# Cross attention on one core: the whole program as one list of words, and the second batch's output in 33 products

## The chip, the cores and the metric

The kernel runs on one core of one Trainium2 chip. A core has five engines that run side by side, each through its own queue of instructions: TensorE (PE; matrix products, its weight loads are listed apart as PEld), VectorE (DVE), ScalarE (ACT), GpSimd (POOL) and SyncE (SP), which here does nothing but issue transfers between DRAM and the on-chip memory SBUF. Products land in PSUM, eight banks of 128 partitions by 512 numbers of 32 bits. The metric is the device time of one execution in microseconds (us).

## What is computed

Two batches of 2048 tokens with 640 channels attend to 154 rows of context with 1024 channels each: 77 of text and 77 of image, with key and value weights of their own and a softmax of their own. There are 20 heads of 32 channels. All is float32.

```python
q = split_heads(x @ Wq.T)
k, v = split_heads(text @ Wk.T), split_heads(text @ Wv.T)
k_ip, v_ip = split_heads(ip @ Wk_ip.T), split_heads(ip @ Wv_ip.T)
out = merge_heads(attend(q, k, v)) + merge_heads(attend(q, k_ip, v_ip))
return out @ Wo.T + bo + x
# attend: softmax(q @ k.T / sqrt(32)) @ v
```

## The kernel before

The matrices lie transposed, with the channels on the 128 partitions. 640 channels are five chunks of 128 (four heads each), 2048 tokens are four blocks of 512 (two halves, `sub`, of two blocks, `h`). A unit `u` (0 to 19) is one batch, one chunk and one half: 1024 tokens in eight groups of 128. It is worked in three groups (`R0`, `R1`, `R2`: three, three and two of the eight).

What a unit does, by the letters that the order of work uses:
- `q` (`queries`, L218): five products of 512 columns into one bank; `cq` (L229) copies it to SBUF.
- `k`, `v` (`project_kv`, L132): keys and values of a chunk, for both batches at once, eight products; `ck`, `cv` copy them. `SQ` (L146) turns v in squares of 32 by VectorE, `VS` (`spread_v`, L152) spreads them over the partitions by 16 small transfers.
- `R` (`scores`, L246), `K` (L261, ScalarE copies the scores into the tile `pb`), `M` (L271, maxima, VectorE), `S` (L277, subtraction, GpSimd), `E` (L283, exponential, ScalarE), `D` (L289, sums and their reciprocals, VectorE), `N` (L297, multiplication, GpSimd), `T` (L303, transposition in squares of 32, VectorE).
- `A` (`attend`, L308): probabilities by values for both halves of a chunk, into four banks; `CA` (L332) copies them into the tile `aT`.

The first batch's output runs between the units of the second batch, the second batch's output after the last attention. For the first 512 output channels and the first 512 input channels it is a scheme of seven products for eight (`product`, L474): channels split in 2 x 2, tokens of a block in halves of 256, with sums of weights (`sum_w`, L365: five, on GpSimd) and of tokens (`sum_t`, L407: four of 512 columns for a block, on GpSimd). Each product is four instructions of 256 columns, four of the seven have two more for the fifth chunk (L491). `take_product` (L500) adds a bank to the residual tile, whose rows were loaded from x, with the bias at the first time. The last 128 output channels are plain products (`last_chunk`, L459, in two parts: `p` ahead of the last attention, the fifth chunk behind it) with `store_last` (L469). In the trace each product is two instructions.

The order of the body is written out as strings, one for each engine and kind of unit (`ORDERS`, L562), merged by a loop that writes a word out as soon as all that it needs has been written (L908). The transfers are issued by SP, one queue, in the order in which the code meets them: the next block of x when a block's last query has been written (`load_next`, L197), eight `VS` transfers behind it, `Wo` and the first residuals behind those of chunk 4 (L168). The last stage is a list by itself (L917 to L939).

Of the kernel before, what the change touches and what calls it, by code (L numbers as in the profile page):

```python
# [19 lines left out]
def kernel(  # L20
# [41 lines left out]
    SCALE = 1.0 / float(D) ** 0.5  # L62
    NP = B * NC
# [50 lines left out]
    loaded, used = [], set()  # L114

    def load_w(upto=len(wlist)):

        while len(loaded) < upto:
            n = len(loaded)
            if n >= len(wslots) and n - len(wslots) not in used:  # L120
                return
            src, c = wlist[n]
            w = wslots[n % len(wslots)]
            nc.sync.dma_start(
                out=w, in_=src[:, ts(c, P)].rearrange("(k p) o -> p k o", p=P)
            )
            loaded.append(w)
# [4 lines left out]
    def project_kv(n, out):  # L132

        load_w()
        t = n % 2
        for k in range(NCC):
            nc.tensor.matmul(  # L137
                keys_in(out), loaded[n][:, k, :], cT[:, k, :, t, :], start=(k == 0), stop=(k == NCC - 1)
            )
        used.add(n)  # L140
# [9 lines left out]
    rest = []  # L150

    def spread_v(q):  # L152


        spread_rest(len(rest))
        for g in range(G):
            for r in range(G):
                rest.append((q, g, r))
        spread_rest(G * G // 2 if q == NC - 1 else None)
        if q == NC - 1:  # L160
            rest.extend(["x", "wo"])

    def spread_rest(n=None):
        for _ in range(len(rest) if n is None else min(n, len(rest))):
            w = rest.pop(0)
            if w == "x" and n is None:
                return
            if w == "wo":  # L168
                nc.sync.dma_start(out=wo, in_=WoT.rearrange("(c p) o -> p c o", p=P))
                for part in PARTS:  # L170
                    fetch(0, part)
            if w in ("x", "wo"):
                continue
            q, g, r = w
            nc.sync.dma_start(  # L175
                out=v4s[q % 2][r * D : (r + 1) * D, g].rearrange("p k d -> p (k d)"),
                in_=squares(q)[g * D : (g + 1) * D],
            )
# [18 lines left out]
    def load_next(u, h):  # L197

        _, b, c, _ = step_of(u)
        n = place_of(u, h)  # L200
        if b == 0 and (c < NC - 1 or n == XROOM):
            return
        m = late.index((u, h)) + XROOM if b else n
        if m < len(late):
            v, g = late[m]
            tokens = ds(S + (step_of(v)[3] * NH + g) * TB, TB)
            nc.sync.dma_start(out=xs[n], in_=xT[:, tokens].rearrange("(k p) t -> p k t", p=P))
            spread_rest()
# [20 lines left out]
    def take_queries(u, h, pq):  # L229
        qT = qpool.tile([P, TB], F32, tag="qT", name=f"qT_{u}_{h}")  # L230
        nc.scalar.copy(qT, pq)  # L231
        qTs[(u, h)] = qT
# [38 lines left out]
    def maxima(u, s):  # L271
        n = GROUPS[s][1] * G
        mx = small.tile([P, n, 2], F32, tag=f"mx{n}", name=f"mx_{u}_{s}")
        nc.vector.tensor_reduce(mx, rows_of(u, s), AX.X, ALU.max)  # L274
        maxs[s] = mx

    def subtract(u, s):  # L277
        n = GROUPS[s][1] * G
        nc.gpsimd.tensor_tensor(  # L279
            rows_of(u, s), rows_of(u, s), maxs[s].unsqueeze(3).to_broadcast([P, n, 2, L]), ALU.subtract  # L280
        )

    def exponential(u, s):  # L283
        e = keys_of(u, s).rearrange("p n g l -> p (n g) l")
        nc.scalar.activation(e, e, AF.Exp, scale=SCALE)  # L285
# [3 lines left out]
    def sums(u, s):  # L289
# [5 lines left out]
        rdens[s] = rden  # L295

    def normalise(u, s):  # L297
        n = GROUPS[s][1] * G
        nc.gpsimd.tensor_tensor(  # L299
            rows_of(u, s), rows_of(u, s), rdens[s].unsqueeze(3).to_broadcast([P, n, 2, L]), ALU.mult  # L300
# [225 lines left out]
    for k in (0, half):  # L526
# [4 lines left out]
        load_w(k // half + 1)  # L531
    for _ in range(NH * NC):
        load_x()
    load_w()
# [11 lines left out]
    for t in range(2):  # L546
# [3 lines left out]
        for b in range(B):  # L550
            nc.scalar.copy(kT[:, 0, b, t, :], keys_in(ps)[:, b])

    ORDERS = {  # L562
        "0": (
            "1010", "430",
            "R0 R1 R2 F2 F0 F1",
            "K0 K1 K2 E0 E1 E2 C0 C2 C1",
            "M0 C0 M1 M2 D0 D1 D2 T0 C2 C1",
            "S0 S1 S2 N0 N1 N2",
        ),
        "1": (  # L570
            "1000", "26647",
            "F0 R0 R1 F3 F2 R2 F4 F1",
            "C0 K0 K1 K2 C2 E0 C3 C4 E1 E2 C1",
            "SQ M0 M1 T1- C3 C4 M2 T2- D0 D1 C0 D2 T0 C2 C1",
            "S0 S1 S2 N0 N1 N2",
        ),
        "even": (
            "1101", "310",
            "R2 R0 F2 R1 F0 F1 AT",
            "K2 K0 K1 E0 C0 C2 E1 C1 E2 CA",  # L580
            "C0 M0 T1- M1 T2- M2 D0 C2 C1 D1 D2 T0",
            "S0 S1 S2 N0 N1 N2",
        ),
        "odd": (
            "0010", "05244",
            "R0 F3 F0 R2 R1 F4 F2 F1",
            "K0 C3 C0 K2 K1 E0 C2 E2 C4 E1 C1",
            "M0 C4 C1 T1- M2 M1 SQ C2 D0 T2- D2 C0 C3 D1 T0",
            "S0 S2 S1 N0 N2 N1",
        ),  # L590
        "8": (
            "1100", "502",
            "R2 R0 F1 R1 F2 F0 AT",
            "K2 K0 K1 C2 C1 E0 C0 E2 E1 CA",
            "M2 C1 M0 T2- T1- M1 C0 D0 D2 D1 T0 C2",
            "S2 S0 S1 N0 N2 N1",
        ),
        "9": (
            "1101", "020",
            "R0 F0 R2 R1 F2 F1",  # L600
            "C0 K0 K2 K1 E0 E2 C1 C2 E1",
            "SQ M0 T2- C1 C2 M2 M1 D0 T1- C0 D2 D1 T0",
            "S0 S2 S1 N0 N2 N1",
        ),
        "10": (
            "1001", "4110",
            "F1 R0 R2 F0 R1 AT F2 F3",
            "C1 K0 K2 C0 K1 CA E0 E2 E1",
            "T2- T1- M0 M1 M2 D0 C2 C3 D1 D2 T0",
            "G1 W0 S0 S2 S1 N0 W1 N1 N2",  # L610
        ),
        "11": (
            "1100", "335421",
            "R0 F1 R1 R2 F3 F2 F4 F0 F5",
            "K0 C1 K1 K2 E0 C0 E1 E2",
            "M0 C3 M1 M2 C4 T1- C2 D0 T2- D1 C5 D2 T0",
            "S0 G2 S1 G3 S2 N0 N2 N1 G4",
        ),
        "12": (
            "0000", "7605",  # L620
            "R1 F0 F2 R0 F1 R2 F3 AT",
            "K1 K0 C0 C1 K2 E0 E1 CA E2",
            "C2 T2- M0 T1- M1 C3 M2 D0 D1 T0 D2",
            "S0 S1 S2 N0 G1 N1 N2",
        ),
        "13": (
            "0011", "560574",
            "F1 R0 F3 R1 R2 F2 F4 F5 F0",
            "K0 C1 K1 K2 E0 E1 E2 C0",
            "C3 M0 M1 M2 C2 T2- D0 D1 C5 D2 C4 T0 T1-",  # L630
            "S0 S1 S2 N0 N1 N2 G3",
        ),
        "14": (
            "0000", "6540",
            "R2 F0 R1 F2 R0 F1 AT F3",
            "K2 K1 K0 C1 E2 E0 CA E1 C0",
            "M2 T1- T2- M0 M1 C2 D2 D0 C3 D1 T0",
            "S2 G2 S0 S1 G4 N0 N2 N1",
        ),
        "15": (  # L640
            "0000", "071365",
            "F5 R0 F4 R2 F2 R1 F1 F3 F0",
# [329 lines left out]
```

## Time and profile before

| what | us |
|---|---|
| median of three runs (lowest, highest) | 509.31 (509.28, 510.11) |
| span of the profiled execution | 506.7 |
| its time outside the span | not recorded for this execution; the median is 2.6 above the span |
| first query product starts | 4.4 |
| last attention starts, ends | 431.3, 436.8 |
| first output product behind it starts | 437.12 |
| last matmul ends | 502.97 |

How to read the profile: the page gives, for one execution, the busy time of each engine. "By stretches" cuts the span; a row has the busy time of TensorE, the weight loads, VectorE, ScalarE and GpSimd with their instructions in brackets, then the granted clock and the DMA share. The chain of work that ended last is followed back from the end; its pieces have a start and a length. The timeline merges neighbours of the same line: start, length from the first start to the last end, engine, line, operation, output<-inputs, shape, number. VectorE's and GpSimd's own lengths overlap a little with the next instruction's, so the distance from start to start is what one costs in a row.

### The profile page before, as it was taken

To read this page: it belongs to the slowest core of one execution; us is meant where nothing else is said; L and a number is where in the kernel's file an instruction comes from. 1 tells how busy PE (TensorE), PEld (TensorE's weight loads), DVE (VectorE), ACT (ScalarE), POOL (GpSimd) and SP (SyncE) were. 2 spreads that over 40 slices of the span, in tenths; PEclk is the share of its full clock that TensorE was granted. 3 is DMA by queue.
4 is the path that set the end of the run, shared out by engine and by line. 5 is a ranking of instruction groups with operands and counts; after the bars stand their busy time and mean duration, and the time that the engine had idled before them with its cause. 6 is when DMAs were issued, how large, how long until landed. Compare 5 with 4: busy or idle time off the path is not lost.

```text
span 506.7 us, 10153 instructions
## 1 busy us (share of the span) xinstructions
PE 498.3 (98%) x4270; PEld 321.0 (63%) x4270; DVE 391.9 (77%) x347; ACT 242.5 (48%) x423; POOL 395.0 (78%) x163
## 2 busy tenths in 40 slices
PE   9999999999999999999999999999999999999997
PEld 5657557557656565456565656554755775588885
DVE  0079999999899987958997997699899999333333
ACT  1266666666676566645545636454654750100000
POOL 0079999989989988899999997798899999940000
PEclk9999999999999999999999999999999999999999
DMA  8982621331362453885574485168323242641213
GB/s 274 357 210 61 159 69 46 86 92 46 92 185 74 112 198 116 284 314 145 159 237 124 131 260 158 53 178 292 110 72 95 86 162 65 225 147 62 84 41 104
DMA packets 71053, 73.03 MB, mean 144 GB/s; under 512 B 5600, under 2 KB 50912, under 8 KB 71008
## 3 DMA queue, kind: packets, MB, share of 16 engines
q1 hardware_dynamic: 70288, 71.67, 45.9%
q8 instruction: 33, 0.54, 0.5%
q10 hardware_dynamic: 720, 0.72, 0.4%
q14 instruction: 12, 0.10, 0.1%
HBM read 58.61 MB, written 10.49 MB: 136 GB/s over the span
## 4 chain that ended last, share of the span: by engine, by line
PE 86%; DMA 5%; POOL 4%; DVE 1%; SPq 1%; issue 1%; ACT 0%; DVEq 0%; POOLq 0%
PE bank L221 31%; PE bank L481 18%; PE bank L253 9%; PE bank L315 9%; PE bank L137 9%; PE bank L461 5%; PE bank L491 5%; DMA x<-in_x_dram 3%; DMA wo_ct<-in_L_xattn_Wo_dram 2%; POOL pb L299 2%; POOL pb L279 1%; SPq L175 1%; POOL x L384 1%; DMA acc<-in_x_dram 1%; PE bank L541 1%
## 5 line engine op out<-in xcount | busy, mean ns | idle before, releaser
L279 POOL TENSOR_TENSOR pb<-pb,mx 128x1848 f32<-128x1848 f32 (+1 forms) x60 | 175.4, 2941 | 45.3 <-DVE mx L274 45.1
L221 PE MATMUL bank<-x,wq 128*128 128x512 f32 x400 | 180.7, 601 | 0.1
L299 POOL TENSOR_TENSOR pb<-pb,rden 128x1848 f32<-128x1848 f32 (+1 forms) x60 | 175.0, 2939 | 5.2 <-DVE rden L294 5.2
L274 DVE TENSOR_REDUCE mx<-pb 128x24 f32<-128x1848 f32 (+1 forms) x60 | 109.6, 1845 | 33.0 <-ACT pb L265 32.8
L265 ACT COPY pb<-bank 128x462 f32<-128x462 f32 (+1 forms) x240 | 101.7, 535 | 59.3 <-PE bank L253 58.5
L221 PEld LDWEIGHTS bank<-x,wq 128*128 128x128 f32 x400 | 74.1, 191 | 85.0 <-issue 81.7
L292 DVE TENSOR_REDUCE den<-pb 128x24 f32<-128x1848 f32 (+1 forms) x60 | 110.4, 1840 | 17.3 <-ACT pb L285 16.9
L285 ACT ACTIVATE pb<-pb 128x1848 f32<-128x1848 f32 (+1 forms) x60 | 94.9, 1582 | 56.4 <-POOL pb L279 56.2
L306 DVE STREAM_TRANSPOSE pb<-pb 128x1920 f32<-128x1920 f32 (+1 forms) x60 | 114.8, 1923 | 2.1 <-POOL pb L299 2.1
L253 PEld LDWEIGHTS bank<-kT,qT 32*128 32x128 f32 x1280 | 47.4, 184 | 26.3 <-issue 18.0
L253 PE MATMUL bank<-kT,qT 32*128 32x154 f32 x1280 | 58.7, 306 | 0.7 <-ACT vT L899 0.4
L315 PE MATMUL bank<-pb,v 32*32 32x512 f32 x1600 | 55.8, 597 | 1.2 <-ACT pb L265 0.7
L481 PE MATMUL bank<-aT,wo_ct 128*128 128x256 f32 x192 | 47.6, 382 | 1.0 <-DVE acc L512 0.7
L137 PEld LDWEIGHTS bank<-wo_ct,aT 128*128 128x128 f32 x320 | 43.1, 188 | 4.2 <-issue 3.5
L315 PEld LDWEIGHTS bank<-pb,v 32*32 32x32 f32 x1600 | 30.7, 103 | 23.2 <-issue 11.8
L137 PE MATMUL bank<-wo_ct,aT 128*128 128x154 f32 x320 | 45.3, 295 | 0.0
L481 PEld LDWEIGHTS bank<-aT,wo_ct 128*128 128x128 f32 x192 | 36.0, 190 | 11.0 <-issue 3.8
L231 ACT COPY qT<-bank 128x512 f32<-128x512 f32 x40 | 23.1, 588 | 31.4 <-PE bank L221 31.4
L461 PE MATMUL bank<-aT,wo_ct 128*128 128x512 f32 x80 | 36.1, 597 | 0.0
L506 DVE SCALAR_TENSOR_TENSOR pb<-bank,bo_sb,pb 128x256 f32<-128x256 f32 x24 | 10.5, 479 | 26.9 <-PE bank L491 16.4
L491 PE MATMUL bank<-aT,wo_ct 128*128 128x256 f32 x96 | 28.6, 379 | 0.0
L506 DVE SCALAR_TENSOR_TENSOR acc<-bank,bo_sb,acc 128x256 f32<-128x256 f32 x40 | 17.0, 466 | 13.3 <-PE bank L491 6.6
(47 smaller groups left out, 286.2 us busy)
## 6 DMA issues: line engine op xcount, KB each, us to landing
x<-in_x_dram SPq DMA_DIRECT2D x20, 1280.0 KB, 6.9
x<-in_x_dram SPq DMA_DIRECT2D x21, 256.0 KB, 5.2
out_dram<-acc SPq DMA_DIRECT2D x19, 256.0 KB, 2.8
acc<-in_x_dram SPq DMA_DIRECT2D x16, 256.0 KB, 6.7
v<-vS SPq DMA_DIRECT2D x160, 20.0 KB, 1.8
pb<-in_x_dram SPq DMA_DIRECT2D x3, 1024.0 KB, 7.6
wq<-in_L_xattn_Wq_dram SPq DMA_DIRECT2D x9, 320.0 KB, 4.8
aT<-in_L_xattn_Wk_dram SPq DMA_DIRECT2D x5, 512.0 KB, 5.6
```

The costliest lines, as they stand in the source:

```text
L137: nc.tensor.matmul(keys_in(out), loaded[n][:, k, :], cT[:, k, :, t, :], start=(k == 0), stop=(k == NCC - 1))
L221: nc.tensor.matmul(pq, wqs[q % 3][:, k, :], xs[place_of(u, h)][:, k, :], start=(k == 0), stop=(k == NC - 1),)
L253: nc.tensor.matmul(ps[g][:, ts(t, 2 * L)], qTs[(u, h)][g * D : (g + 1) * D, ts(st, P)], kT[g * D : (g + 1) * D, c, b].rearrange("p t l -> ...
L265: nc.scalar.copy(keys_of(u, s)[:, :, g], ps[g][:, : n * 2 * L].rearrange("p (n l) -> p n l", n=n))
L274: nc.vector.tensor_reduce(mx, rows_of(u, s), AX.X, ALU.max)
L279: nc.gpsimd.tensor_tensor(rows_of(u, s), rows_of(u, s), maxs[s].unsqueeze(3).to_broadcast([P, n, 2, L]), ALU.subtract)
L285: nc.scalar.activation(e, e, AF.Exp, scale=SCALE)
L292: nc.vector.tensor_reduce(den, rows_of(u, s), AX.X, ALU.add)
L299: nc.gpsimd.tensor_tensor(rows_of(u, s), rows_of(u, s), rdens[s].unsqueeze(3).to_broadcast([P, n, 2, L]), ALU.mult)
L306: nc.vector.transpose(p, p)
L315: nc.tensor.matmul(pa[r][g * D : (g + 1) * D, :], v4s[q % 2][rows, g, k, :], zones[rows, :, g, k, :], start=(k == 0), stop=(k == NK - 1),)
L481: nc.tensor.matmul(part, w_of[m][:, kp, op], t_of(m, b, i)[:, kp], start=(op == kp == 0 and m in (1, 2, 5)), stop=(op == 1 and kp == 1 and ...
```

## The change

All that is in `ORDERS`, `OUTPUT` and the last list becomes one list of words, `SCHEDULE` (953 words), from which each engine's queue and SP's queue are written in that order. A word is one of the steps above with its unit (`R0.5`), `@` gives the bank or half of the banks. Loads are words as well: `LX` a block of x, `LQ` query weights, `LK` key and value weights, `LO` all of `Wo`, `LF` the first residuals. Up to the last attention the words are those of before in a somewhat different order. The scale 1/sqrt(32) moves from the exponential to the copy of the queries. `DIRECT` is empty, so the path for it is never taken.

The second batch's output for the first 512 output channels is a scheme of its own: weights as 4 x 5 squares of 128, tokens in two halves of 1024, 33 products in place of 40 plain ones. A product `F` is one weight square by 1024 tokens, written as two words of 512 columns. 24 weight sums `V` (40 instructions, on VectorE, into the first zone of `pb`) and 25 token sums `X` (1024 columns; 18 on GpSimd, `p`, and 7 on VectorE, `d`). Eight chains of products each gather in one bank per block, and are read on the way by `Y`, which adds or subtracts the bank to or from a residual tile (62 words); a product behind a `Y` goes on in the same bank. `z`, `yz` are the fifth chunk of the last 128 channels and its addition. Three of the four blocks' residuals are the last blocks of x, which still lie in SBUF; the fourth is loaded (`LA`). `LW` loads a part of `Wo` again that the first batch's scheme has overwritten.

The core of the diff:

```diff
@@ take_queries
-        nc.scalar.copy(qT, pq)
+        nc.scalar.mul(qT, pq, SCALE)
@@ exponential
-        nc.scalar.activation(e, e, AF.Exp, scale=SCALE)
+        nc.scalar.activation(e, e, AF.Exp)
@@ the lists
-    ORDERS = {
...
-    written = {None}
-    while any(queues):
...
+    SCHEDULE = (
+        "R0.0@1 R1.0@0 K0.0 K1.0 M0.0 R2.0@1 q.1.1@0 K2.0 LK.5 M1.0 S0.0 LK.4 M2.0 q.1.0@1 S1.0 E0.0 cq.1.1 "
...
+        "T2.0 VS.0.0 K0.2 M2.2 N2.1 M0.2 VS.0.1 N1.1 R1.2@1 T0.1 v.1.0@2 LF T2.1 S2.2 q.4.0@3 cv.1.0 K1.2 "
...
+        "N0.8 cv.4.0 D1.8 CA.3 R0.9@1 v.4.1@0 N2.8 T0.8 K0.9 N1.8 cv.4.1 M0.9 R2.9@0 R1.9@1 K2.9 q.10.1@0 "
+        "SQ.4 S0.9 K1.9 T2.8 VS.4.1 M2.9 M1.9 S2.9 E0.9 VS.4.0 q.11.0@3 T1.8 S1.9 E2.9 LX.12.0 cq.10.1 LO "
...
+        "R0.12@0 cm3.0 q.13.0@5 G5.1 E2.11 cm6.0 K0.12 G7.0 D2.11 N0.11 D1.11 m7.0 LX.14.0 VS.6.1 M0.12 N1.11 "
+        "q.13.1@6 cm7.0 D1.10 T1.11 N1.10 R2.12@0 LQ.9 LQ.8 q.14.0@7 K2.12 T0.11 N2.11 T1.10 m4.0 S0.12 T2.11 "
...
+        "T2.18 p.0@5 cm6.3 D0.19 S2.19 E1.19 D1.19 m7.3 N0.19 E2.19 p.1@4 cm7.3 LW D2.19 N1.19 T0.19 m4.3 "
+        "N2.19 T1.19 p.2@7 X.A.p@0 T2.19 cm4.3 V.P LA A.9@0 V.A V.Q V.G V.O V.M X.D.d@1 X.I.p@2 X.K.d@3 CA.9 "
+        "V.E F31.0@0 V.J V.U F31.1@1 V.T V.F V.L X.U.d@4 F0.0@0 z.2 V.B V.H V.S F0.1@1 V.X F25.1@2 V.R V.D "
+        "V.C z.0 X.S.d@5 z.3 Y6.1.10 X.L.p@6 z.1 yz.0 yz.2 F7.0@3 Y0.0.11 F7.1@5 X.T.p@7 yz.3 F25.0@7 Y0.1.11 "
+        "Y2.1.31 F23.0@0 Y6.0.10 X.O.p@8 F23.1@1 Y0.0.01 F20.1@2 Y2.1.21 Y0.1.01 F20.0@7 X.C.p@9 yz.1 F24.0@0 "
+        "Y6.1.11 F24.1@1 Y6.0.11 F15.1@5 V.N Y2.0.31 X.Q.p@10 F10.0@4 F10.1@6 Y3.0.21 F29.0@7 X.V.d@11 "
+        "F11.0@4 Y3.1.21 X.M.p@12 F1.0@0 Y2.0.21 F11.1@6 Y0.0.00 F29.1@2 Y6.0.21 X.G.p@13 Y3.0.20 F1.1@1 "
+        "Y3.1.20 F13.1@5 F6.0@0 V.V Y0.1.00 X.F.p@0 F15.0@3 Y2.1.11 F3.0@4 Y6.1.21 F13.0@3 X.B.d@4 F3.1@6 V.I "
+        "F30.1@2 Y3.0.00 X.J.p@5 Y3.1.00 F18.0@0 Y6.1.20 F18.1@1 V.W F30.0@7 X.W.d@3 F21.0@4 Y2.0.11 X.N.p@6 "
...
+        "F32.0@0 Y5.0.31 Y1.0.30 F9.1@6 Y1.1.20 F16.0@7 Y4.0.20 F9.0@7 Y5.1.21 Y1.1.30 F28.1@2 Y5.0.21 "
+        "F32.1@2 Y7.0.30 Y4.1.20 "
+    ).split()
@@ the scheme: sums of tokens A.., sums of weights A.., products (weight, tokens), chains
+    R_SUMS = (
+        "+01-21 +30+11 +21-31 +31+11 +10-00 +11-10 +30-31 +30+10 +01-00 +01-11 +01-D +21-I +30+C +G+J +D-I "
+        "+M-20 +20-L +E+N +40-41 +11-41 +11-40 +10-40 +C-40 +C-41 +V+20 "
+    ).split()
+    W_SUMS = (
+        "+01+30 -32-13 +10+02 +34-24 +03-01 +01+20 +30+31 +20-E +D-22 +03-A +13-I -32-02+12 +00-10-20 "
+        "-12-10-13 +00+01+02 +14-04-34 -P-11 +H+22+23 +32-J+33 +Q-22-24 -G-01+21-22 +U+03-23 +13-V-33 "
+        "+01-Q-03-21+22+23 "
+    ).split()
+    PRODUCTS = (
+        "04 41, 02 Q, K C, M 00, 30 E, B M, L 20, 34 S, W 30, D X, "
+        "H K, F O, A R, N 21, J N, P T, R D, G F, 11 V, S G, "
+        "Q U, O I, E J, C L, 04 S, T 40, I W, 32 P, U H, X 11, "
+        "V B, 10 A, 22 Y"
+    ).split(", ")
+    CHAINS = (
+        "0,31:+11 23:+01 1,24:+00 6,18:+10",
+        "4:-00 17:-20-30",
+        "7:-21-31 13,15:-11",
+        "10:+21 11:+20 3:+00 21:+01",
+        "14:-31 12:+00 28,32:+20",
+        "22:+01+31 9,16:+21",
+        "25:-10 20:-11 29:-21 30:-20 8:-30 19:-31",
+        "26:-21 2:-11 5:-31 27:-10-30",
+    )
...
+        n = int(text)
+        if n < 2:
+            flat = xs[XROOM].rearrange("p k t -> p (k t)")[:, ts(n, NH * TB)]
+        elif n < 4:
+            return aT[:, ds(NC * NHB + 2 * (n - 2), NH)]
+        else:
+            flat = pb_flat[:, ds(zone + (n - 4) * NH * TB, NH * TB)]
...
+    def add_part(o, ps, op):
+        t = sum_at(o)
+        if o in untouched:
+            untouched.discard(o)
+            nc.vector.scalar_tensor_tensor(t, t, bo_sb[:, o[0] : o[0] + 1], ps, ALU.add, op)
+        else:
+            nc.vector.tensor_tensor(t, t, ps, op)
...
+            nc.sync.dma_start(out=outT[ts(m, P), ds(S + i * TB, TB)], in_=t)
...
+        elif k == "V":
+            out = weight(args[0])
+            (op, a), *more = terms(W_SUMS[number(args[0])])
...
+                if n == 0 and op == ALU.subtract:
+                    nc.vector.scalar_tensor_tensor(out, weight(a), -1.0, weight(b), ALU.mult, o2)
                 else:
+                    nc.vector.tensor_tensor(out, weight(a) if n == 0 else out, weight(b), o2)
+        elif k == "X":
...
+            (nc.vector if e == "d" else nc.gpsimd).tensor_tensor(places[w], ra, rb, op)
...
+            nc.tensor.matmul(
+                at[(c, h)], weight(w), tokens_of(x)[:, h], start=first, stop=True, skip_group_check=True
+            )
...
+    for word in SCHEDULE:
+        emit(word)
```

A `V` thus reads two squares of weights in SBUF, an `X` two rows of 1024 tokens in SBUF, a `Y` a bank and one tile. Places 4 to 13 of token sums lie in the second and third zone of `pb` (the last attention reads both), places 0 and 1 in the fourth block of x, places 2 and 3 in rows of `aT`. In R_SUMS and PRODUCTS a pair of digits is a chunk and a half of the tokens, in W_SUMS an output and an input chunk.

## The prediction

> **What bounds the kernel now.** I read the busy table, the busy time by stretches of 50 us, the chain that ended last in order of time, and the timeline of the last 90 us.
>
> From the page, and the busy time by stretches (after the stretch: PE, weight loads, VectorE, ScalarE, GpSimd, clock, DMA):
> ```profile
> PE 498.3 (98%) x4270; PEld 321.0 (63%) x4270; DVE 391.9 (77%) x347; ACT 242.5 (48%) x423; POOL 395.0 (78%) x163
> 100.00:150.00 50.00, 50.00 (x603) 31.32 (x602) 46.48 (x36) 33.53 (x59) 45.88 (x17) 1.00 0.38 104
> 200.00:250.00 50.00, 48.62 (x422) 28.37 (x421) 42.23 (x36) 26.59 (x41) 47.37 (x22) 1.00 0.68 220
> 470.00:480.00 10.00, 10.00 (x48) 8.80 (x47) 3.32 (x7) 0.00 (x0) 0.00 (x0) 1.00 0.24 80
> ```
> TensorE is full in every stretch, at full clock. Up to 425 us VectorE and GpSimd are over 90% full as well, so the order has little slack; in the last 65 us VectorE works a third of the time and GpSimd not at all. That is the room which the change uses.
>
> The chain in order of time (start, us, what):
> ```profile
> 198.24 6.54 DMA x<-in_x_dram
> 206.01 9.92 DMA wo_ct<-in_L_xattn_Wo_dram
> 416.71 1.73 PE bank L481 x8
> 424.46 6.87 PE bank L461 x16
> ```
> Eight 256-column instructions take 1.73, one 0.216; sixteen of 512 columns take 6.87, one 0.429. Every product of the program is two instructions here. The first two lines are the only long transfers that the chain leans on in mid-course.
>
> The timeline around the last attention:
> ```profile
> 419.80 0.63 DVE L512 TENSOR_TENSOR acc<-acc,bank 128x512 f32<-128x512 f32 x1
> 420.35 2.06 DVE L292 TENSOR_REDUCE den<-pb 128x24 f32<-128x1848 f32 x1
> ...
> 427.04 3.56 DVE L306 STREAM_TRANSPOSE pb<-pb 128x1920 f32<-128x1920 f32 x2
> ...
> 428.73 2.49 POOL L414 TENSOR_TENSOR x<-aT 128x512 f32<-128x512 f32 x2
> ...
> 431.26 5.52 PE L315 MATMUL bank<-pb,v 32*32 32x512 f32 x160
> ...
> 437.12 1.99 PE L481 MATMUL bank<-aT,wo_ct 128*128 128x256 f32 x8 [0.34 <-ACT aT L342]
> ...
> 449.54 0.88 DVE L506 SCALAR_TENSOR_TENSOR acc<-bank,bo_sb,acc 128x256 f32<-128x256 f32 x2 [0.84 <-issue]
> ```
> VectorE's last transpose ends at 430.60, the last attention runs to 436.8, and from 437.12 TensorE does nothing but output products, to 502.97. After its end come an addition and a store, to 506.7. I call everything from 437.12 on the tail.
>
> The times are of one execution: span 506.7. The median, 509.31, is 2.6 above; I add 2.6 at the end.
>
> **The change, part by part.**
>
> *Products of the tail.* Before: per block of 512 tokens 28 products of 256 columns and 8 fifth pieces, 36; for four blocks 144 x 2 x 0.216 = 62.2. After: 33 x 2 halves of 512 columns = 66 x 2 x 0.429 = 56.6. The four `z`/`o` pieces are in both (3.4). Gain **5.6**. "33 for 40" counts a plain product; against what ran before it is 33 for 36. With the start at 437.1 and 70 pieces of 0.858, TensorE would end at 497.2.
>
> *VectorE in the tail.* It takes over, from 430.6: the last addition of the first batch (0.8); 40 instructions for weight sums (`V`, 128 columns); 7 sums of tokens (`X`, 1024 columns); 62 additions from banks (`Y`), 16 of them with bias, and 4 `yz`.
> - `Y`: 419.80 to 420.35 is 0.55 from start to start; I take 0.57. With bias: the pair at 449.54 takes 0.88, one 0.48, so 0.40 from start to start for 256; 256 columns more at 0.267 (1.985 us for 1848 elements in L274, less the fixed part) give 0.67. Sum 46 x 0.57 + 20 x 0.67 = 39.6.
> - `V` and `X` read two tiles of SBUF, which no VectorE instruction of before does: each has a bank or one tile. Alone, 128 columns are 0.40 less 0.133, 0.27; 1024 columns at L274's pace are 1.1. Low end of `V`: the 128x16 reciprocal, start to start 0.17. High end: the instruction has to wait for a GpSimd sum beside it, 2.47 for 1024 columns (428.73 to 431.18). I take 0.27 and 1.1, the rows nearest in kind, and one wait where a run of them meets a GpSimd sum. 40 x 0.27 + 7 x 1.1 = 18.5.
>
> In all 58.9, to 489.5 without waits: 7.7 less than TensorE. But the start is tight. Product 7 needs `X.S`, behind 32 `V` instructions and 4 `X`: 431.4 + 8.6 + 4.4 = 444.4. TensorE has nine pieces ahead of it, 437.1 + 9 x 0.858 = 444.8. GpSimd goes from `X.A` straight into `X.I` (to 433.7), so `V.P` starts at 433.7 and `X.S` ends at 446.7: TensorE waits **1.9**.
>
> *Later sums on VectorE.* `V.N`, `X.V`, `X.B`, `V.V`, `V.I`, `V.W`, `X.W`, `V.K` stand in seven runs among GpSimd's sums: 0 to 7 x 2.47 = 17 of waiting, half of it 8.6, against 7.7 of slack: **+1.0**.
>
> *GpSimd in the tail.* 18 sums of 2.47 are 44.5, to 473 if unbroken; `X.X` feeds product 9 at 493. Cover 20. Its places 4 to 13 lie in the zones that the last attention reads, so `X.L` cannot start before 436.8.
>
> *Banks.* A chain goes on accumulating in its bank after `Y` has read it. In the list two other pieces (1.7) or more stand between most such pairs, and `Y` is 0.6: no cost, as long as VectorE isn't behind.
>
> *End.* Last product, then one 512-column addition and a store of 256 KB in place of two halves of 128 KB; landings are 2.2 and 1.8: **+0.4**.
>
> *The body.* Same instructions: the scale moves from the exponential to the copy of the queries, both of which pass an activation already. On TensorE the same items stand between one attention and the next in the first batch (37.1 us from the one at 69.37 to that at 106.46, all of it busy), so the order can win only the gaps. Those lie at 205 to 240 us: 1.4 by the second stretch above. There `wo` was issued at 206.0, behind eight `v` transfers (198.67 to 205.30) and the next block of x. In the new queue `LO` stands right behind `LX.12.0`, with all 16 `v` transfers ahead of both: 191.2 + 16 x 0.63 = 201.3 and 0.4 for the block, so 201.7, 4.3 earlier; the first residuals (`LF`) go out ahead of the first attention and don't share its landing. GpSimd's 2.6 of waiting for `wo` goes with it; what is late next is TensorE's own work. I take **-1.2**. A block that waits for its slot holds what is behind it in SP's queue, the `VS` transfers among them; `LX.14.0` has 6.8 us from its slot to its use (`m7.0` 1.7, `q.13.1` 4.3, `R2.12` 0.7) and such a block lands in 6.9 (median). That is the place with least slack; up to +3.
>
> *Loads of the tail.* Three of four residual loads go (the blocks of x lie there); `LW` and `LA` are issued ahead of the last attention, 10 us before use against 6 to 7 of landing. Nothing.
>
> **Sum:** -5.6 + 1.9 + 1.0 + 0.4 - 1.2 = -3.5. Span 503.2, time **505.8**.
>
> One rule speaks against this. By the Trainium skill (SBUF — State Buffer, Who interferes with whom) a VectorE instruction with two SBUF inputs and a GpSimd instruction that reads SBUF exclude each other for a whole instruction, while one with a single SBUF input does not. The trace agrees with the second half (the pair of L506 takes 0.88 at 439.20 beside a GpSimd sum and 0.88 at 449.54 with GpSimd idle) and cannot show the first. Taken strictly, with turns, it gives the first rival's time; without it, the second's.
>
> **Rivals.**
> 1. *Slower: the weight sums and GpSimd take turns.* Place: from 436.8 to `X.S`. GpSimd then has eight sums ready (`L T O C Q M G F`); the ninth, `X.J`, needs the place of `X.S`. If each goes ahead of one VectorE sum, `X.S` is 8 x 2.47 = 19.8 later and TensorE stands; with 3 more in the later runs: 503.2 + 19.8 + 3 = 526, time **528.6**. It decides from the second extra sum on: 3.5/2.47 = 1.4. For: GpSimd's sums follow each other without a gap (428.73, 431.18), nothing in the list holds them back. Against: a run of back-to-back `V` may keep its turn.
> 2. *No interference:* 1.9 and 1.0 go: **502.9**.
> 3. *The body slips:* three engines over 90% full and one new order; the `LX` chain of SP late by up to a landing (6.9): 505.8 + 3 to 7, about **510**.
> 4. *It doesn't do what it says:* 33 for 36 is sure from the list; that TensorE isn't the bound of the tail any more would be rivals 1 or 3.
>
> **Chances.** Forecast 0.40 (504 to 508); rival 1 0.35 (513 to 530); rival 2 0.15 (501.5 to 504); rival 3 0.10 (508 to 513). A measurement of this kernel tells about 0.2% from no change. Faster: 0.15 + 0.37 = 0.52; within 0.2%: 0.06; slower: 0.42. The two signs are near each other, so the range reaches from 501.5 to 530; the forecast's own is 504 to 508.
>
> **What would show it.** Tail start near 436; product pieces at 0.858 without gaps but for one of 2 ahead of product 7; `V` at 0.27, `X` at 1.1 on VectorE. Wrong, if `V` rows have means of 1 us and more and TensorE waits for VectorE by 10 or more between 441 and 466 (rival 1); if the last attention starts later than 432 (rival 3); if 205 to 240 still has its gaps, the body's -1.2 falls.

## The result, and the profile after

The change makes the kernel **slower: 540.98 us** (median of four executions, 538.12 to 542.03) against 509.68 for the kernel before on the same chip (509.28 to 510.11). The ratio is **1.061, 95% interval 1.058 to 1.064**. That is outside the range of the prediction (501.5 to 530). The profiled execution took 538.12, its span is 536.3.

From the page of the changed kernel, the busy table and the granted clock in 40 slices of 13.4 us:
```profile
PE 502.1 (94%) x4114; PEld 294.1 (55%) x4114; DVE 452.8 (84%) x412; ACT 242.4 (45%) x423; POOL 421.0 (78%) x165
PEclk9999999999999999999999999999999998589799
```
TensorE has fewer instructions (4114 for 4270), but its busy time is not shorter, and four slices at the end have a lower clock (8, 5, 8 and 7 tenths). Both belong together: at half clock the same instruction counts as busy for twice as long.

Busy time by stretches of the changed kernel (PE, weight loads, VectorE, ScalarE, GpSimd, clock, DMA):
```profile
425.00:450.00 25.00, 23.01 (x211) 12.01 (x209) 24.36 (x26) 4.87 (x10) 21.45 (x9) 1.00 0.30 94
450.00:475.00 25.00, 11.83 (x17) 4.60 (x18) 24.58 (x31) 0.00 (x0) 13.29 (x6) 0.66 0.08 31
475.00:500.00 25.00, 21.85 (x51) 9.19 (x49) 23.52 (x30) 0.00 (x0) 20.11 (x8) 1.00 0.03 11
500.00:537.00 37.00, 30.58 (x64) 13.16 (x64) 26.29 (x41) 0.00 (x0) 0.66 (x1) 0.88 0.31 114
```
In the second row TensorE does 17 instructions in 25 us, and VectorE is full: 24.58 us for 31 instructions, 0.8 each, though most of them are weight sums of 128 columns. VectorE has become the engine that everything waits for.

The timeline of VectorE in the tail shows why (start, us, what):
```profile
437.68 2.58 DVE L812 TENSOR_TENSOR pb<-wo_ct 128x128 f32<-128x128 f32 x1
440.30 0.29 DVE L812 TENSOR_TENSOR pb<-pb,wo_ct 128x128 f32<-128x128 f32 x1
...
444.57 2.44 DVE L812 TENSOR_TENSOR pb<-wo_ct 128x128 f32<-128x128 f32 x1
446.94 2.43 DVE L812 TENSOR_TENSOR pb<-wo_ct,pb 128x128 f32<-128x128 f32 x1
...
451.74 9.35 DVE L812 TENSOR_TENSOR pb<-pb,wo_ct 128x128 f32<-128x128 f32 x4
...
466.27 1.80 DVE L812 TENSOR_TENSOR pb<-pb,wo_ct 128x128 f32<-128x128 f32 x6
...
468.39 1.22 DVE L818 TENSOR_TENSOR pb<-aT 128x1024 f32<-128x1024 f32 x1
```
and GpSimd's in the same time:
```profile
437.73 2.39 POOL L818 TENSOR_TENSOR aT<-aT 128x1024 f32<-128x1024 f32 x1
443.66 5.55 POOL L818 TENSOR_TENSOR pb<-aT 128x1024 f32<-128x1024 f32 x2 [3.55 <-DVE x L818]
449.18 2.38 POOL L818 TENSOR_TENSOR pb<-x,aT 128x1024 f32<-128x1024 f32 x1
...
479.50 2.35 POOL L818 TENSOR_TENSOR pb<-aT 128x1024 f32<-128x1024 f32 x1 [16.20 <-PE bank L832]
```
The same operation of 128x128 takes 0.28 where GpSimd is idle (440.1 to 443.7, and from 463.3) and 2.4 where GpSimd has a sum. Between 444.57 and 463.36 eight weight sums pass, one for each of GpSimd's eight sums `L T O C Q M G F`. A shared tile is not the cause: the first row's sum reads `wo_ct` and writes `pb`, GpSimd's beside it (437.73) works on `aT` alone, and the sum takes 2.58 all the same. Then GpSimd stands for 16.20 us, since `X.J` goes to the place of `X.S`, which TensorE has not read yet, and the other weight sums pass at 0.2 to 0.33 from start to start.

What TensorE makes of it:
```profile
461.14 2.08 PE L832 MATMUL bank<-aT,pb 128*128 128x512 f32 x2 [12.75 <-DVE pb L812]
...
469.67 3.39 PE L832 MATMUL bank<-pb,wo_ct 128*128 128x512 f32 x4 [2.03 <-DVE pb L818]
...
502.00 6.54 PE L832 MATMUL bank<-aT,pb 128*128 128x512 f32 x8 [3.65 <-DVE aT L818]
```
It waits 12.75 us for a weight sum, 2.03 for `X.S`, and later 3.65 for `X.W`. In the last row the instructions start 0.85 apart up to 507.3, twice the 0.429: in the tail the granted clock is 0.5 from 453.14 to 466.80, from 470.21 to 473.62 and from 500.93 to 507.76, each time in or behind a pause.

The tail also starts late. The ten attentions begin at 70.3, 107.4, 144.5, 185.1, 221.6 ... 438.0; before it was 69.3, 106.4, 143.5, 180.6, 214.6 ... 431.3. So 6.7 of the 31 us are lost ahead of the tail, and 6.0 are added at the fourth and fifth attention. The 1.0 ahead of the first says nothing of the order: a run below with the old body has it too (70.4). TensorE's pauses, with the instructions behind them:
```profile
171.53 4.53 PE L191 MATMUL bank<-x,wq 128*128 128x512 f32 x10 [1.91 <-DMA x<-in_x_dram]
185.11 8.03 PE L311 MATMUL bank<-pb,v 32*32 32x512 f32 x160 [1.46 <-DMA v<-vS]
216.13 4.53 PE L191 MATMUL bank<-x,wq 128*128 128x512 f32 x10 [3.12 <-DMA x<-in_x_dram]
```
The middle row is the fourth attention itself. It takes 8.03 us where the others take 5.52: the clock is 0.5 from 186.90 to 190.32, behind a pause of only 1.46, and this costs 1.7; for the rest it waits on the way for more `v` transfers. All three wait for transfers, and the queue that issues them shows what they stood behind:
```profile
157.61 4.94 SPq L148 DMA_DIRECT2D v<-vS  x8
...
163.22 0.58 SPq L176 DMA_DIRECT2D x<-in_x_dram  x1
...
176.51 32.42 SPq L148 DMA_DIRECT2D v<-vS  x24
209.04 0.53 SPq L176 DMA_DIRECT2D x<-in_x_dram  x1
209.61 0.52 SPq L154 DMA_DIRECT2D wo_ct<-in_L_xattn_Wo_dram  x1
```
`LX.10.0` goes out at 163.22, behind `VS.3.1` (before: 160.45, ahead of all `v` transfers); `LX.12.0` at 209.04, behind 16 transfers of `VS.4` (before: 198.24, between the two eights). `wo` goes out at 209.61, where the prediction had 201.7. The merged row of 24 hides a wait: the eight of `VS.3.0` are out by 185.3, then the queue stands until 198.94 for VectorE's squares `SQ.4`, and the 16 of `VS.4` follow at 0.63 each. VectorE's row after and before:
```profile
198.58 0.56 DVE L142 STREAM_TRANSPOSE vS<-vT 128x160 f32<-128x160 f32 x2
```
```profile
190.86 0.57 DVE L148 STREAM_TRANSPOSE vS<-vT 128x160 f32<-128x160 f32 x2 [1.24 <-ACT vT L899]
```

### The profile page after: what moved, and what is told of

Read it like the earlier page. It is cut to its first block, busy times and chain, and to the rows that moved or that the text cites. A ratio compares the mean times of both kernels' runs of the same rounds, so it can differ in the third digit from the quotient of the medians.

```text
span 536.3 us, 9855 instructions
## 1 busy us (share of the span) xinstructions
PE 502.1 (94%) x4114; PEld 294.1 (55%) x4114; DVE 452.8 (84%) x412; ACT 242.4 (45%) x423; POOL 421.0 (78%) x165
## 4 chain that ended last, share of the span: by engine, by line
PE 64%; DVE 13%; DMA 9%; POOL 5%; SPq 4%; issue 2%; ACT 1%; ACTq 0%; DVEq 0%; POOLq 0%
PE bank L191 23%; PE bank L832 8%; PE bank L311 7%; PE bank L223 7%; PE bank L477 7%; DVE pb L812 6%; DMA x<-in_x_dram 6%; PE bank L132 5%; PE bank L457 3%; SPq L148 3%; POOL pb L275 3%; POOL pb L295 2%; PE bank L487 2%; DVE pb L302 2%; DMA v<-vS 2%
## 5 line engine op out<-in xcount | busy, mean ns | idle before, releaser
L223 PEld LDWEIGHTS bank<-kT,qT 32*128 32x128 f32 x1280 | 45.7, 184 | 25.7 <-issue 18.2
L311 PE MATMUL bank<-pb,v 32*32 32x512 f32 x1600 | 57.8, 614 | 1.5 <-DMA v<-vS 1.5
L311 PEld LDWEIGHTS bank<-pb,v 32*32 32x32 f32 x1600 | 32.6, 104 | 22.6 <-issue 9.7
L201 ACT ACTIVATE qT<-bank 128x512 f32<-128x512 f32 x40 | 23.5, 598 | 42.9 <-PE bank L191 42.7
L832 PE MATMUL bank<-aT,pb 128*128 128x512 f32 x44 | 25.2, 699 | 16.4 <-DVE pb L812 12.8
L457 PE MATMUL bank<-aT,wo_ct 128*128 128x512 f32 x80 | 38.0, 622 | 0.0
L477 PE MATMUL bank<-aT,wo_ct 128*128 128x256 f32 x128 | 32.3, 386 | 0.0
L818 POOL TENSOR_TENSOR pb<-aT 128x1024 f32<-128x1024 f32 x6 | 15.0, 2512 | 20.0 <-PE bank L832 16.4
L779 DVE TENSOR_TENSOR x<-x,bank 128x512 f32<-128x512 f32 x36 | 23.5, 682 | 5.4 <-PE bank L832 5.2
L477 PEld LDWEIGHTS bank<-aT,wo_ct 128*128 128x128 f32 x128 | 23.6, 190 | 7.6 <-issue 4.6
```

The source lines that it names most:

```text
L223: nc.tensor.matmul(ps[g][:, ts(t, 2 * L)], qTs[(u, h)][g * D : (g + 1) * D, ts(st, P)], kT[g * D : (g + 1) * D, c, b].rearrange("p t l -> ...
L311: nc.tensor.matmul(pa[r][g * D : (g + 1) * D, :], v4s[q % 2][rows, g, k, :], zones[rows, :, g, k, :], start=(k == 0), stop=(k == NK - 1),)
L477: nc.tensor.matmul(part, w_of[m][:, kp, op], t_of(m, b, i)[:, kp], start=(op == kp == 0 and m in (1, 2, 5)), stop=(op == 1 and kp == 1 and ...
```

## The experiments

The theory after the result: (1) the body is late because of those transfers; (2) in the tail VectorE's sums of two SBUF tiles and GpSimd's sums take turns, an instruction for an instruction; (3) TensorE's pauses halve its clock, which costs again. In the expectations of the first runs theory A is (1) and (2); their D has the numbers of a kernel in which the place of GpSimd's sums makes no difference; other letters are rivals that the quoted texts give numbers for. Every run is compared with the kernel before on its own chip (508.83 to 509.39; for the changed kernel it was 509.68), so where two runs lie close, their ratios are the fairer comparison.

**Half of the change each.** The first run has the new list up to the last attention and the tail of before, the second the other way round:
```diff
 # e1                                   # e2
- SCHEDULE = new body + new tail        - SCHEDULE = new body + new tail
+ SCHEDULE = new body                   + SCHEDULE = old body + new tail
+ the tail's code of before
```


> The new list up to the last attention, and behind it the old tail (36 units of products, its sums on GpSimd). Theory A (two losses: the body's new queue of transfers costs 6.7, as the last attention starts at 438.0 for 431.3; the tail's turns between VectorE and GpSimd, with the half clock after TensorE's pauses, cost the other 24 to 25): 509.7 + 6.7 = 516.4, between 514 and 518. Theory B (the body is as good as before, and its late attention only the queue of the tail's loads in front of it): 509 to 511.

Measured: **516.47**, ratio 1.015 (1.012 to 1.018).

> The old order of the body, written as one list, and behind it the new tail of 33 products. Theory A: 541 - 6.7 = 534.3, between 532 and 537; product 7 waits for a VectorE sum as in the whole change, and TensorE's clock halves after that. Theory B: the whole loss stays, 540 to 542. A theory C (the new tail suffers because the body leaves VectorE and GpSimd late and out of step): under 520, with no VectorE sum of 128 columns over 1 us.

Measured: **531.62**, ratio 1.046 (1.042 to 1.050), 0.4 under the interval expected. The body costs 7.5, the tail 22.6. The product of the two ratios is 1.062, that of the whole change 1.061: the halves add up within their intervals, and no third place is needed.

**GpSimd held.** One added word: a one-column sum on GpSimd that reads `X.S`, so that GpSimd begins its eight sums only when VectorE's burst is over. First in the whole change, then with the old body.
```diff
+        elif k == "H":
+            a = (weight(args[0][1]) if args[0][0] == "w" else places[args[0]][:, 0])[:, :1]
+            nc.gpsimd.tensor_tensor(held, a, a, ALU.add)
- z.3 Y6.1.10 X.L.p@6
+ z.3 Y6.1.10 H.S X.L.p@6
```


> The whole change, with one GpSimd addition of a single column put ahead of X.L; it reads X.S, so GpSimd's eight long sums wait until VectorE is through with its first 32 weight sums. Theory A (a VectorE sum with two inputs in SBUF and a GpSimd sum take turns, one for one): the eight VectorE sums of 2.3 to 2.4 us between 444 and 463 fall back to 0.2, X.S is done near 450 for 469.5, TensorE's pause of 12.8 shrinks to under 2 and the half clock behind it goes; GpSimd is 8 later for the rest and some sums of VectorE wait there: 515 to 522. Theory D (the weight sums are slow by themselves, or wait for transfers or for TensorE): they stay at 2.3 to 2.4, 538 to 543.

Measured: **525.07**, ratio 1.032 (1.030 to 1.034): 16 under the change, 3 to 10 short of what A expected.

> Both: the old order of the body, and GpSimd held until X.S is done. Theory A: the sum of the two, 6.7 below the run with GpSimd held in the new body: 508 to 515, so about the time of the kernel before. Theory D: 532 to 537.

Measured: **518.39**, ratio 1.019 (1.017 to 1.020), 13.2 under the second run, and 3.4 above A's interval. To add idle time to GpSimd makes the kernel faster, so D falls. What A missed is in VectorE's timeline of the second of the two, behind the burst:
```profile
456.37 2.32 DVE L811 TENSOR_TENSOR pb<-pb,wo_ct 128x128 f32<-128x128 f32 x1
...
465.67 3.34 DVE L811 TENSOR_TENSOR pb<-pb,wo_ct 128x128 f32<-128x128 f32 x2
...
479.44 3.35 DVE L817 TENSOR_TENSOR aT<-pb,aT 128x1024 f32<-128x1024 f32 x1
```
and behind the last of them TensorE's:
```profile
482.85 7.05 PE L834 MATMUL bank<-aT,pb 128*128 128x512 f32 x10 [5.86 <-DVE aT L817]
```
The late weight sums `N V I W K`, put among the additions out of PSUM, each still wait a turn. The additions themselves do not: they stay at 0.60 to 0.66 beside GpSimd.

**The late sums made early.** The same kernel (old body, GpSimd held), with those eight instructions moved to where GpSimd is idle:
```diff
- V.R V.D V.C z.0 X.S.d@5 ... V.N ... V.V ... V.I ... V.W ... V.K
+ V.R V.D V.C z.0 V.N V.V V.I V.W V.K X.S.d@5 ...
```


> The run with the body of before and the new tail, GpSimd held until X.S is done (518.39 us), and now the five sums of weights that stood between the additions out of PSUM (N, V, I, W, K: 8 VectorE instructions of 128x128) stand ahead of X.S, where GpSimd is idle. In the run without this each of them took 0.7 to 2.3 us beside GpSimd's sums, 13.7 us in all, against 0.2 to 0.3 alone. Theory T (VectorE instructions with both inputs in SBUF and GpSimd's take turns, each waiting for a whole one of the other): the 8 cost 2.2 us ahead of X.S and give back about 11, but of TensorE's pauses behind them (0.9 + 1.7 + 0.7 + 2.0 + 6.0 us) only those that end on a weight go: 508 to 514, with V rows of 0.2 to 0.33 throughout and X.V, X.B, X.W still at 1.6 to 3.4. Rival L (the remaining pauses come from GpSimd's own late sums, which the hold moved back): 517 to 521.

Measured: **509.73**, ratio 1.001 (0.999 to 1.003). 8.7 us for the place of eight instructions that take 2.2 alone. It is the middle of ten executions: two of 506.0 and 506.9 with a mean clock of 1.0, eight of 509.4 to 510.8 with 0.995 to 0.997. What is left of TensorE's pauses:
```profile
447.69 3.47 PE L834 MATMUL bank<-pb,wo_ct 128*128 128x512 f32 x4 [2.75 <-DVE pb L817]
...
463.59 1.12 PE L834 MATMUL bank<-pb 128*128 128x512 f32 x2 [1.27 <-DVE x L777]
...
476.53 4.56 PE L834 MATMUL bank<-aT,pb 128*128 128x512 f32 x10 [0.66 <-DVE aT L817]
```

**The queue.** The run with the new body and the old tail, with three moves on the queue of transfers and none on an engine:
```diff
- VS.3.1 ... LX.10.0 ... LX.10.1 ... LX.11.1 ... LX.11.0 VS.3.0 ... VS.4.1 ... VS.4.0 ... LX.12.0
+ LX.10.0 VS.3.1 ... LX.10.1 VS.3.0 ... LX.11.1 ... LX.11.0 ... VS.4.1 ... LX.12.0 VS.4.0
```


> The run with the new body and the tail of before (516.47 us, against 508.99 for the kernel before), with three groups of transfers moved on the queue and nothing else: the first block of the second batch's x (LX.10.0) goes ahead of the eight transfers VS.3.1 instead of behind them, VS.3.0 goes ahead of LX.11.1 and LX.11.0 instead of behind them, and LX.12.0 goes between VS.4.1 and VS.4.0 instead of behind both. The order on the engines stays that of the change. Theory Q (the body is late because x and v are issued late on the one queue; the pauses of TensorE at 169.6, 183.7 and 213 in the changed kernel each end on such a transfer): 508.5 to 512, with the fourth attention near 181 and the fifth near 215. Rival O (the new order of TensorE and VectorE itself is slower, and the transfers are only what ends last): 514 to 517, with the pauses still there behind another releaser.

Measured: **509.79**, ratio 1.002 (1.000 to 1.005), from 516.47. The queue of this kernel:
```profile
155.79 0.58 SPq L176 DMA_DIRECT2D x<-in_x_dram  x1
157.49 6.62 SPq L148 DMA_DIRECT2D v<-vS  x8
...
195.26 4.94 SPq L148 DMA_DIRECT2D v<-vS  x8
200.30 0.53 SPq L176 DMA_DIRECT2D x<-in_x_dram  x1
200.88 6.71 SPq L148 DMA_DIRECT2D v<-vS  x8
```
`LX.10.0` goes out 7.4 earlier than in the changed kernel, `LX.12.0` 8.7 earlier. The fifth attention begins at 215.0 (expected: near 215), the fourth at 183.6 only (expected: near 181). The three pauses are gone, but the moves made a new one ahead of the fourth attention, for value weights: their load went out at 168.32 in the changed kernel, and now goes out at 173.68, behind `VS.3.0`.
```profile
181.34 2.35 PE L132 MATMUL bank<-wo_ct,aT 128*128 128x154 f32 x16 [1.85 <-DMA aT<-in_L_xattn_Wv_dram]
```
`wo` goes out at 207.63, still later than before (206.01), so its place was not what cost the time. The new order on the engines itself costs less than 0.5%, and gains nothing that shows. The ten executions reach from 507.8 to 513.6; the two above 513 have the lowest mean clock (0.992, the others 0.995 and more).

**Smaller pieces.** The whole change, with the eight sums of GpSimd cut in four:
```diff
- (nc.vector if e == "d" else nc.gpsimd).tensor_tensor(places[w], ra, rb, op)
+ # for w in "LTOCQMGF": four instructions of 128x256 instead of one of 128x1024
```


> The whole change, with GpSimd's eight sums of 128x1024 that met the burst of weight sums (L, T, O, C, Q, M, G, F) each issued as four of 128x256. The same work, 32 instructions of about 0.6 us instead of 8 of 2.35. Theory T (turns, one instruction of each engine for one of the other, whatever its length): the 22 weight sums between X.K and X.S each wait for one quarter, 0.6 to 0.7 us instead of eight at 2.4 and fourteen at 0.3; X.S is done 7 to 10 us earlier, TensorE's pause of 12.8 us shrinks to 2 to 5, and the time falls to 523 to 534. Rival B (the two share the port by time or bytes, so that GpSimd gets its 19 us first whatever the pieces): X.S stays within 1.5 us and the time within 538 to 543.

Measured: **533.41**, ratio 1.048 (1.043 to 1.052); 7.6 under the change with the same work in more instructions. VectorE's timeline, where rows with a count take together what is shown:
```profile
446.14 0.82 DVE L812 TENSOR_TENSOR pb<-wo_ct 128x128 f32<-128x128 f32 x1
...
448.46 2.89 DVE L812 TENSOR_TENSOR pb<-pb,wo_ct 128x128 f32<-128x128 f32 x4
...
458.90 3.62 DVE L812 TENSOR_TENSOR pb<-pb,wo_ct 128x128 f32<-128x128 f32 x5
```
Now every weight sum of the burst takes 0.7 to 0.8, not eight of them 2.4 and the rest 0.3. So a turn is an instruction, whatever its length, and not a share of time. The first pause of TensorE shrinks from 12.75 to 1.44, but the wait for `X.S` grows from 2.03 to 11.31: together 2.0 less. Behind the two pauses TensorE works 3.3 us at half clock instead of 9.1, which is 2.9 us less; the rest was not taken apart. `X.S` is done 4.8 earlier counted from the start of the tail, where 7 to 10 was expected.

**The clock.** The whole change, with products that nobody uses in TensorE's three longest pauses, first 28 + 4 + 8 of them, then half:
```diff
+        elif k == "U":
+            for _ in range(int(args[0])):
+                nc.tensor.matmul(banks[int(where)], weight("00"), tokens_of("00")[:, 0], start=True, stop=True)
- F25.1@2 ... F7.0@3 ... F26.0@5
+ U.28@2 F25.1@2 ... U.4@3 F7.0@3 ... U.8@5 F26.0@5
```


> The whole change, with matrix instructions of 512 columns that compute nothing that is used, put on TensorE where it paused longest: 28 ahead of F25.1 (the pause of 12.8 us), 4 ahead of F7.0 (2.0 us) and 8 ahead of F26.0 (4.2 us). They write banks that the next product overwrites. Theory H (TensorE's clock is halved because it paused, and comes back only some us after it works again): the granted clock stays at 1.0 in the tail, no product takes 0.85, and the time falls by the half-rate stretches that are not inside a later wait, 1.7 + 2.9 us: 534 to 538. Rival N (the low clock does not come from the pause, or costs nothing because VectorE's additions are the limit): 540 to 542; if the dummies are slower than planned and delay the products, 542 to 546.

Measured: **546.08**, ratio 1.071 (1.068 to 1.075). A miss by a wrong count: each product is two instructions, as the prediction itself had said, so the filling was twice as long as the pause and the next product came 11 us later in the tail. The mean clock of the run rose from 0.973 to 0.993, and in the tail it is 1.00 up to the last product, so the half clock does come from the pauses; its price cannot be read here.

> The earlier run with idle products in TensorE's pauses gave 546.08 us, since each 512-column product is two instructions of 0.429 us, so that 28 of them filled 24.0 us of a pause of 12.8 and the next product came 12 us late; the granted clock stayed at 1.0 through the tail all the same. Now half as many: 14 ahead of F25.1, 2 ahead of F7.0, 4 ahead of F26.0. Theory H (the pause is what halves the clock, and the half-rate stretches behind 470 and 502 us cost 1.7 + 2.9 us that nothing hides): clock at 1.0 in the tail and 534 to 538 us. Rival N (the half clock is hidden behind VectorE and GpSimd, which are late anyway): clock at 1.0 and 539.5 to 542.

Measured: **536.83**, ratio 1.056 (1.053 to 1.058), 4.2 under the change in microseconds, 2.9 by the ratios. The time is in H's interval, its condition is not met: the pause ahead of `X.S` was still 3.1, and the clock was 0.5 from 469.65 to 476.48 behind it. So the price of all of the half clock is not shown.

**Both mended.** The whole change with the queue's three moves, GpSimd held and the late sums early (all diffs as above):

> The whole change with both things mended that the runs so far point to: the three groups of transfers moved on the queue (alone: 509.79 with the tail of before, 0.9 over the kernel before), GpSimd held until X.S is done and the five late weight sums ahead of X.S (alone: 509.73 with the body of before, 0.9 over). If body and tail add up: 509.5 to 512, the same as before within the measurement, and 30 us under the change. If the two have a cause in common that shows only together (the queue at 205, a later start of the tail): over 513.

Measured: **510.78**, ratio 1.003 (1.002 to 1.004). This is in the interval for two losses that add up. The ratio falls from 1.061 to 1.003 with one instruction added and eight words of the list moved. The new pause for value weights is here too: 3.13 us in the profiled execution, the slowest of the six (512.99), with 3.4 us of half clock from 181.71.

**The first pause.** Two more moves in the tail: `X.I` on VectorE, and `X.S` ahead of the burst.
```diff
- X.D.d@1 X.I.p@2 X.K.d@3 CA.9 V.E F31.0@0 V.J V.U F31.1@1 ... X.S.d@5 ... H.S
+ X.D.d@1 X.I.d@2 X.K.d@3 X.S.d@5 CA.9 V.E F31.0@0 V.J V.U F31.1@1 ... H.wK      # first
+ X.D.d@1 X.I.d@2 X.K.d@3 CA.9 V.E F31.0@0 V.J V.U X.S.d@5 F31.1@1 ... H.wK      # then, old body
```


> As the run with both mended, and X.I goes to VectorE (1.2 us, so that the second instruction of V.P no longer waits 2.1 us beside it), X.S goes ahead of the burst of weight sums, right behind X.K, and GpSimd is held until V.K, the last of the weight sums. By the turns: 0.9 us less at the first wait, and F7.0 no longer ends TensorE's first pause, which the trace has at 2.9 us with 1.6 us of half clock behind it: 507.5 to 510. If TensorE waits at the next product instead, for a bank that VectorE empties only behind the burst: 509.5 to 512.

Measured: 506.85, ratio 0.996 (0.994 to 0.997). It is no fair time: `X.S` reads a row that the last attention fills, and here it is summed before that, from older data.

> The run with the body of before, GpSimd held and the five late weight sums early (509.73 us), with the two moves of the last step: X.I on VectorE, X.S ahead of the burst, GpSimd held until V.K. In the run before this one X.S stood ahead of the taking of the last attention, so that it summed one row of older data, and the taking then waited for it: the first product came 1.7 us later than it need. Here X.S stands behind that, after V.U. By the turns and the pauses of TensorE in the run without the two moves (2.9 us at 444 with 1.6 us of half clock behind it, 0.9 us at the first wait): 503.5 to 506, 1% under the kernel before, and no V row above 0.4 us. If only the place of the wait changes (a bank that VectorE empties behind the burst): 508 to 510.

Measured: **509.19**, ratio 0.999 (0.997 to 1.001): the second guess, not the first. `X.S` no longer ends the pause, a bank does, which VectorE empties only behind the burst. But its twelve executions fall into two groups: five with a mean clock of 1.00 at 506.4 to 508.2 (middle 507.1), seven with 0.995 to 0.997 at 509.1 to 510.5 (middle 510.0). The profiled one is of the second group; two stretches of its tail, and the products behind the pause:
```profile
425.00:450.00 25.00, 21.49 (x196) 9.36 (x195) 23.58 (x55) 2.31 (x8) 8.27 (x6) 0.97 0.22 75
450.00:475.00 25.00, 24.46 (x55) 10.41 (x53) 22.66 (x27) 0.00 (x0) 24.84 (x11) 0.96 0.08 31
```
```profile
448.40 1.90 PE L834 MATMUL bank<-pb,wo_ct 128*128 128x512 f32 x2 [3.12 <-DVE res L775]
450.08 1.92 PE L834 MATMUL bank<-aT,pb 128*128 128x512 f32 x2
```
Two instructions that take 1.02 elsewhere take 1.90 here. The last run puts three idle products into that pause:
```diff
- yz.2 F7.0@3
+ yz.2 U.3@3 F7.0@3
```


> The last run (509.19 us, ratio 0.9991 to the kernel before), with 3 products that nobody uses put ahead of F7.0, into the bank that F7.0 overwrites. In that run TensorE paused for 3.3 us behind F7.0, and then worked at half rate for some executions: its twelve executions fall into five with a mean clock of 1.00 (506.4 to 508.2, middle 507.1) and seven with 0.995 to 0.997 (509.1 to 510.5, middle 510.0). Theory H (a pause of 3 us is what halves the clock, and what follows it costs 2.9 us): the pause falls to 0.7 to 1.0, every execution has a clock of 0.999 or more in its mean, and the median is 506.4 to 507.6, ratio 0.994 to 0.997. Rival N (the two groups differ by something else, and the clock only goes with it): the two groups stay, 508.5 to 510. If the idle products hold up F7.0 by more than the pause: 510 to 511.

Measured: **507.04**, ratio 0.9965 (0.9954 to 0.9977), all nine executions between 506.41 and 507.61 with a clock of 0.999 or 1.0. It is the version that beats both kernels. The same rows:
```profile
425.00:450.00 25.00, 24.07 (x203) 10.64 (x202) 23.59 (x54) 2.31 (x8) 8.29 (x5) 1.00 0.19 64
450.00:475.00 25.00, 25.00 (x59) 10.87 (x58) 23.10 (x32) 0.00 (x0) 24.92 (x11) 1.00 0.11 42
```
```profile
449.15 1.12 PE L837 MATMUL bank<-pb,wo_ct 128*128 128x512 f32 x2 [0.55 <-DVE res L775]
450.12 1.02 PE L837 MATMUL bank<-aT,pb 128*128 128x512 f32 x2
```
The product behind the pause comes at the same point of the tail (12.0 us behind its start in both), so the idle products took no wait away. The median is that of the faster group of the run before (507.1): what has gone is the slower group. Between the two traces the tail is 3.2 us shorter: 1.7 at once, four instructions at 0.85 for 0.43, and most of the rest two later pauses (0.54 and 0.65) that are gone; why those go too was not followed.

## Why the prediction was wrong

*Its likeliest case chose the wrong end of one unknown.* The step that failed is the price of the weight sums: "I take 0.27 and 1.1, the rows nearest in kind, and one wait where a run of them meets a GpSimd sum". Alone they do take 0.20 to 0.33, and 1.14. Beside GpSimd the burst did not pay one wait but eight. The high end was in the text, as the first rival, with its place, its eight sums by name and `X.J` as the end of it; the trace shows each of these. The argument against, that a run of back-to-back sums may keep its turn, falls: VectorE gets one instruction, GpSimd the next, as long as both have one ready. The Trainium skill (SBUF — State Buffer, Who interferes with whom) had the exclusion for a whole instruction. The prediction's trace could show only its second half; the runs now show the first too: 2.4 for 0.28 with two SBUF inputs, and 0.60 to 0.66 either way for the additions that read one SBUF tile and a bank.

*The later sums:* +1.0 was forecast as half of the turns (8.6 of 17) less 7.7 of slack. With GpSimd held, VectorE's rows show 10.0 us of waiting at the eight weight sums (12.2 from start to start for 2.2 alone; the 13.7 in the quoted expectation is too high) and 3.2 at the three token sums: nearly all the turns. Moving just the weight sums away brought 8.7 of the 10.0, so hardly any slack was there: a weight sum that waits also holds up the additions behind it on VectorE, and these hold TensorE's banks.

*The first wait*, 1.9 for `V.P` behind `X.I`: the mechanism is right (2.58 in the first row of VectorE's timeline), it was lost in the larger one.

*The body.* -1.2 was +6.7. The failed step is in "191.2 + 16 x 0.63 = 201.3 and 0.4 for the block, so 201.7, 4.3 earlier". The start was wrong: the 191.2 of the old kernel became 198.94, since VectorE's squares came 7.7 later and the queue stood for them. And the sum priced `wo`, not the block of x in front of it: `LX.12.0` had gone out at 198.24, between the eights; by the prediction's own count it would go out at 201.3, it did at 209.04, and TensorE stood 3.12 for it. With `LX.12.0` between the eights again, and `LX.10.0` and `VS.3.0` ahead, the body is back to 1.002 (1.000 to 1.005), so no more than 0.5% is left for everything else in it. The prediction saw that risk as its third rival, but looked for it at `LX.14.0`.

*The clock was in no case.* The first rival's 528.6, with 7.9 for the body (6.7 and the 1.2 that did not come), is 536.5; measured was 541.0. The difference, 4.5, is near to what the run with half-filled pauses gained (4.2, or 2.9 by the ratios). In its tail TensorE worked 14.8 us at half clock, up to 7.4 us more than at full clock, some of it hidden ahead of the next wait; and the body's 6.7 holds 1.7 of half clock, at the fourth attention. How much of the whole the clock cost was not shown. By the Trainium skill (TensorE: Matmul & The Clock Gate, Part 1: The HAM clock gate) TensorE falls to half clock after an idle window of about 3.4 us and comes back after as long a busy one. The traces agree as far as they go: half clock began 4.7 us after TensorE had stopped at 448.4 and ended 5.7 after it had started again, and with a pause of 3.1, a little under the page's figure, seven of twelve executions show it in their mean clock. Shorter pauses set it off as well: the 1.46 at 185.11 and the 2.03 at 469.67 each have 3.4 us of half clock behind them, the 1.91 at 171.53 and the 3.12 at 216.13 have none. So a pause under 3.4 is not safe here, and its length alone does not decide; what else does was not followed.

*What held:* 70 pieces of 0.858; additions at 0.60 and 0.66 (forecast 0.57 and 0.67); no pause for a chain's bank as long as VectorE keeps up. Of the 5.6 saved on products the best version keeps 1.9: its tail, from the first product after the last attention to TensorE's end, is 63.9 long, before it was 65.9.

## What to carry to other kernels

Before work goes from one engine to an idle one, list which instructions of the two read two SBUF tiles at the same time; price each by a whole instruction of the other engine, not by its own length, and put them where the other is idle or cut the long ones. In a list that orders the transfers too, walk each transfer that TensorE waits for back through the queue, and count what is ahead of it, in issue time, in the new list and not in the old. A pause of TensorE can cost more than itself: half clock followed pauses of 1.46, 2.03 and 3.65 us as well as the one of 12.75, though not every pause.

## What the runs showed of the hardware that was not expected

- Turns are strict and go by instructions: in the changed kernel GpSimd ran at 2.35 from start to start, as alone (2.32 in the run with the old body and GpSimd held, with VectorE on other work), while VectorE's instructions of 0.28 went at the same pace; with pieces of 256 columns both went at 0.74. The one with the long instructions loses nothing. Only where VectorE's sum is long too does GpSimd feel it: 3.2 to 3.4 for its 2.35 beside a sum of 1.2.
- A sum of 128 columns that reads the result of the one before starts 0.32 behind it, an independent one 0.20.
- Idle products can make a kernel faster: three of them, 2.6 us of TensorE's time in a pause of 3.1, brought the ratio from 0.999 to 0.9965 (509.19 and 507.04 us) and took the spread of the executions from 4.1 to 1.2 us.
